# The first 18 key slots of a Perceiver cross attention: keys projected in quarters, queries in small pieces

## The chip, the cores and the metric

The kernel runs on one core of a Trainium2 chip. The metric is the device time of one execution in microseconds (us), the median of several runs. A core has five engines that matter here: TensorE (PE in the profile, with PEld for its weight loads), VectorE (DVE), ScalarE (ACT), GpSimd (POOL), and SyncE (SP), whose queue issues most of the transfers.

## What is computed

The program is one block of a Perceiver: cross attention from 512 tokens to a context of 8192, then a windowed self attention, then a mixture of experts. Only the first part is touched. Cut to that:

```python
x: (2, 512, 512)   ctx: (2, 8192, 512)   mask: (2, 1, 1, 8192)   # float32; 16 heads of 32
def xattn(query, key, value, mask, Wq, bq, Wk, bk, Wv, bv, Wo, bo):
    q, k, v = query @ Wq.T + bq, key @ Wk.T + bk, value @ Wv.T + bv
    q, k, v = split_heads(q), split_heads(k), split_heads(v)
    att = einsum('bhqd,bhkd->bhqk', q, k) / sqrt(32)
    att = where(mask == 0, -inf, att)
    out = einsum('bhqk,bhkd->bhqd', softmax(att, axis=-1), v)
    return merge_heads(out) @ Wo.T + bo
x = x + xattn(layernorm(x), ctx, ctx, mask, ...)
x = x + window_attention(layernorm(x), ...)
x = x + experts(layernorm(x), ...)
```

## The kernel before

**Units, slots and rounds.** The cross attention is cut into 8 units: 2 batches by 4 groups of 4 heads (4 x 32 = 128 rows of the array). A unit goes through the 8192 context tokens in 16 chunks (NKC) of 512 tokens (KC). Unit by unit, chunk by chunk, this gives 128 slots (NS). The main loop (L399) runs over slots, and each slot has four rounds `i`, one for each 128 queries of the batch.

A softmax needs the maximum of a row of scores before its exponentials. The kernel makes it in a pass of its own, ahead: `max_part(s, c)` (L265) computes the scores of 128 queries by 512 keys for four heads and reduces them to one maximum per query and head. The second pass, `scores` and `values` (L323, L348), begins LAG = 18 slots later. So slots 0 to 17 hold the first pass only: key projections, scores with their maxima, and the query projections that later units need. That stretch is what the change is about.

**max_part in the early slots** (L271 to L290). A score tile `sx` is two PSUM banks (2 x 512 float32), and a round uses two of them, from a pool `pairs` of three. Four float32 matmuls (L276) multiply the four heads in four strips of 32 rows of the array; four small bfloat16 matmuls (L282) subtract the mask's row, in the same tiles. Two VectorE reductions (L287), one a tile, then take the maxima. Only after that is a tile free for the next scores.

**project_k(slot, half)** (L230) projects half a chunk of keys: 16 matmuls with 32 columns of weights each, so that the four heads of the group lie in four 32-partition strips of one PSUM tile `pk`, and one ScalarE instruction (L243) adds the bias and writes `kt`. Rounds 0 and 1 of a slot do one half each (L421), after the round's `max_part`. The keys of a slot are scored in the slot after it.

**query(b, g)** (L170) projects the 512 queries of one batch for one group: four matmuls with 128x128 weights and 512 tokens (L173), and one ScalarE instruction (L177). `query_norm(b)` takes the layer norm's statistics on VectorE, and `query_in(b, c)` normalizes 128 tokens (L90), transposes them on TensorE (L98) and copies them out of PSUM on ScalarE (L99). For batch 0 the inputs and the first group come ahead of the loop (L387 to L390). All the rest is a list `later` of 12 calls, of which round 3 of slots 1 to 12 takes one each (L423).

**mask_rows** (L183) turns the mask into a bias and into rows: one VectorE instruction, two TensorE transposes, small ScalarE copies, and three small transfers to memory that ScalarE issues. SP then loads such a row, spread over 128 partitions, for each slot (L221). The first of these loads waits until the row has been written.

**PSUM.** It has eight banks. In the early slots the pool `ps` has two of them, for all of keys, queries, transposes and the maximum's column, and `pairs` has six. From slot 18 on, one pool of eight takes their place (L402).

**Order.** Each engine works through its own instructions in one order, and a framework adds the waits. That order is nearly the code's. The framework also gives out buffers, and it may put an instruction ahead of earlier ones on its engine where it reckons that those can't start yet: the statistics of batch 1, which the list asks for in slot 4, start at 18.77 us in the trace. Loads of the context (`load`, L204) are asked for one slot ahead and run up to three ahead, since four buffers take them; SP waits for a buffer at its head and holds what is behind it.

The pieces that set the order around the change:

```python
load(0); load_x(1); wv_sb = load_w(wv, cp, "wv_sb")
query_norm(0); [query_in(0, c) for c in range(4)]; query(0, 0)
mask_rows(); load_mask(0)
for slot ...:                       # L399
    for i in range(4):
        max_part(slot - 1, i)       # then scores, values from slot 18 on
        if i < 2: project_k(slot, i)
        if i == 3 and slot > 0 and later: later.pop(0)()
        if i >= 2 and slot >= NKC: project_v(slot, i - 2)
    # at a unit's last chunk: max_finish
```

Of the kernel before, what the change touches and what calls it, by code (L numbers as in the profile page):

```python
# [10 lines left out]
F32 = mybir.dt.float32  # L11
# [3 lines left out]
AF = mybir.ActivationFunctionType  # L15
ALU = mybir.AluOpType
AX = mybir.AxisListType
PSUM = bass.MemoryType.PSUM

P = 128  # L20
B, S, D = 2, 512, 512
T = B * S
S2 = 8192
H, DK = 16, 32
G = 4
DC = D // P
# [8 lines left out]
KC = 512  # L35
NKC = S2 // KC
# [7 lines left out]
def perceiver_kernel(  # L44
# [8 lines left out]
    nc = tc.nc  # L53
# [8 lines left out]
    def load_x(b):  # L62
        nc.sync.dma_start(
            out=x_sb[:, ts(b, NT // B), :],
            in_=x[ts(b, S), :].rearrange("(n p) d -> p n d", p=P),
        )
# [27 lines left out]
    def transposed(dst, src, ps):  # L94

        tp = ps.tile([P, 4, P], F32, tag="ps", name="tp")
        for c in range(4):
            nc.tensor.transpose(tp[:, c, :], src[:, ts(c, P)], ident)  # L98
        nc.scalar.copy(dst, tp)  # L99
# [17 lines left out]
    with ExitStack() as es:  # L117
        cp = es.enter_context(tc.tile_pool(name="a_const", bufs=1))
        tmp = es.enter_context(tc.tile_pool(name="a_tmp", bufs=2))
# [3 lines left out]
        pp = es.enter_context(tc.tile_pool(name="a_p", bufs=4))  # L123
        dram = es.enter_context(tc.tile_pool(name="a_dram", bufs=1, space=bass.MemoryType.DRAM))

        first_ps = ExitStack()
        ps = first_ps.enter_context(tc.tile_pool(name="a_ps1", bufs=2, space=PSUM))
        pairs = first_ps.enter_context(tc.tile_pool(name="a_pairs", bufs=3, space=PSUM))

        def load_w(src, pool, tag):  # L130
            t = pool.tile([P, DC, D], F32, tag=tag, name=tag)
            nc.sync.dma_start(out=t, in_=src.rearrange("(c p) f -> p c f", p=P))
            return t

        bq_c = cp.tile([P, G], F32, name="bq_c")
# [15 lines left out]
        nc.vector.memset(mrep, 0.0)  # L151
        junk = cp.tile([P, KC], BF16, name="junk")

        wq_sb = load_w(wq, pp, "p")
        wk_sb = load_w(wk, cp, "wk_sb")


        qT = cp.tile([P, G, T], F32, name="qT")
        xnT, ln = {}, {}

        def query_norm(b):
            ln[b] = layernorm_stats(tmp, range(b * (NT // B), (b + 1) * (NT // B)))
            xnT[b] = pp.tile([P, DC, S], F32, tag="p", name="xnT")

        def query_in(b, c):
            xn = tmp.tile([P, D], F32, tag="row", name="xn")
            normalized(xn, b * (NT // B) + c, *ln[b])
            transposed(xnT[b][:, :, ts(c, P)], xn, ps)

        def query(b, g):  # L170
            pq = ps.tile([P, S], F32, tag="ps", name="pq")
            for c in range(DC):
                nc.tensor.matmul(  # L173
                    pq, lhsT=wq_sb[:, c, ts(g, P)], rhs=xnT[b][:, c, :],
                    start=(c == 0), stop=(c == DC - 1),
                )
            nc.scalar.activation(qT[:, g, ts(b, S)], pq, AF.Identity, bias=bq_c[:, g : g + 1])  # L177

        mbias = cp.tile([P, B, S2 // P], F32, name="mbias")
        mrow = dram.tile([B, S2 // P, P], F32, name="mrow")  # L180
# [2 lines left out]
        def mask_rows():  # L183


            nc.vector.tensor_scalar(mbias, mask_i, 0.0, -BIG, ALU.is_equal, ALU.mult)
            for b in range(B):
                tp = ps.tile([P, P], F32, tag="ps", name="tpk")
                nc.tensor.transpose(tp[0 : S2 // P, :], mbias[:, b, :], ident)
                mt = tmp.tile([S2 // P, P], F32, name="mt")  # L190
                nc.scalar.copy(mt, tp[0 : S2 // P, :])
                nc.scalar.dma_start(out=mrow[b], in_=mt)
                if b == 0:
                    mh = tmp.tile([S2 // P, P], BF16, name="mh")
                    nc.scalar.mul(mh, tp[0 : S2 // P, :], -1.0)
                    nc.scalar.dma_start(out=mrow_h, in_=mh)
# [3 lines left out]
        NS = len(chunks)  # L200
# [3 lines left out]
        def load(slot):  # L204

            for b, j in {(units[u][0], j) for u, j in wanted(slot)}:
                t = ctxp.tile([P, DC, KC], F32, tag="ctx", name="ctx_t")
                nc.sync.dma_start(
                    out=t, in_=ctxT[b, :, ts(j, KC)].rearrange("(c p) s -> p c s", p=P)
                )  # L210
                ctx_t[slot, b] = t

        def load_mask(slot):

            u, j = chunks[slot]
            early = slot + 1 < LAG
            t = mp.tile(
                [P, KC], BF16 if early else F32, tag="mkh" if early else "mk", name="mk", bufs=3
            )
            rows = mrow_h if early else mrow[units[u][0]]  # L220
            nc.sync.dma_start(  # L221
                out=t,
                in_=rows[ts(j, KC // P), :].rearrange("c p -> (c p)").partition_broadcast(P),
            )
            mk_t[slot] = t
# [1 line left out]
        def wanted(slot):  # L227
            return [chunks[s] for s in (slot, slot - NKC) if 0 <= s < NS]

        def project_k(slot, half):  # L230
            u, j = chunks[slot]
            b, g = units[u]
            if half == 0:
                k_t[slot] = kp.tile([P, KC], F32, tag="k", name="kt")
            hs = ts(half, KC // 2)
            pk = ps.tile([P, KC // 2], F32, tag="ps", name="pk")
            for c in range(DC):
                for h in range(4):
                    nc.tensor.matmul(  # L239
                        pk[ts(h, DK), :], lhsT=wk_sb[:, c, ds(g * P + h * DK, DK)],  # L240
                        rhs=ctx_t[slot, b][:, c, hs], start=(c == 0), stop=(c == DC - 1),
                    )
            nc.scalar.activation(k_t[slot][:, hs], pk, AF.Identity, bias=bk_c[:, g : g + 1])  # L243
# [61 lines left out]
        def max_finish(u):  # L305


            rest = ps.tile([P, 4, 4], F32, tag="ps", name="mcol")
            nc.vector.tensor_reduce(rest, mst[u], AX.X, ALU.max)
            for i in range(3):  # L310
                nc.vector.tensor_copy(mrep[:, :, :, i], rest)
                if i < 2:
                    nc.vector.tensor_tensor(rest, rest, mrep[:, :, :, i], ALU.subtract)
            pm = ps.tile([P, S], F32, tag="ps", name="pm")
            for c in range(4):
                nc.tensor.matmul(
                    pm[:, ts(c, P)], lhsT=mrep[:, c, :, :].rearrange("p h r -> p (h r)"),
                    rhs=ident_h, start=True, stop=True,
                )
            m_t[u] = mp.tile([P, S], BF16, tag="mT", name="mT")  # L320
            nc.scalar.copy(m_t[u], pm)
# [60 lines left out]


        load(0)
        load_x(1)
        wv_sb = load_w(wv, cp, "wv_sb")
        query_norm(0)  # L387
        for c in range(NT // B):
            query_in(0, c)
        query(0, 0)  # L390
        mask_rows()
        load_mask(0)
        later = [lambda g=g: query(0, g) for g in range(1, G)]
        later += [lambda: query_norm(1)]
        later += [lambda c=c: query_in(1, c) for c in range(NT // B)]
        later += [lambda g=g: query(1, g) for g in range(G)]

        waiting = None
        for slot in range(NS + LAG):  # L399
            if slot == LAG:  # L400
                first_ps.close()
                ps = es.enter_context(tc.tile_pool(name="a_ps", bufs=8, space=PSUM))  # L402
            if slot + 1 < NS + NKC:
                load(slot + 1)
            elif slot + 1 == NS + NKC:
                wo_sb = load_w(wo, ctxp, "ctx")
                wqkv_t = [load_w(wqkv[:, ts(i, D)], ctxp, "ctx") for i in range(3)]
            if slot + 1 < NS:
                load_mask(slot + 1)
            s = slot - LAG  # L410
            for i in range(4):
                if 1 <= slot <= NS:
                    max_part(slot - 1, i)
                if s >= 0:
                    scores(s, i)
                if waiting is not None:
                    values(*waiting)
                waiting = (s, i) if s >= 0 else None
                if s >= NKC and chunks[s][1] == 1:
                    finish(chunks[s][0] - 1, i)  # L420
                if i < 2 and slot < NS:  # L421
                    project_k(slot, i)
                if i == 3 and slot > 0 and later:  # L423
                    later.pop(0)()
                if i >= 2 and NKC <= slot < NS + NKC:
                    project_v(slot, i - 2)
            if 1 <= slot <= NS and chunks[slot - 1][1] == NKC - 1:
                max_finish(chunks[slot - 1][0])
# [23 lines left out]
    ps = ctx.enter_context(tc.tile_pool(name="c_ps", bufs=8, space=PSUM))  # L452
# [21 lines left out]
    xnT, aT, hT = {}, {}, {}  # L474
# [468 lines left out]
```

## Time and profile before

| | before |
|---|---|
| median of 3 runs | 3846.05 us |
| lowest and highest | 3838.11 and 3847.68 us |
| profiled execution, its own time | 3841.49 us |
| its span in the profile | 3839.5 us |
| its mean granted TensorE clock | 0.993 |
| VectorE, ScalarE, GpSimd busy | 60%, 41%, 54% of the span |
| first scores of slot 1 (start) | 25.63 us |
| first scores of slot 16 | 224.66 us |
| first scores of slot 18 | 259.93 us |

A page of the profile shows one execution: busy time by engine, the span in 40 slices, the chain that ended last, and groups of instructions by line. The trace behind it can be asked for the instructions in order of time, for who waited for whom, and for busy time and granted clock in any stretch. A group's line gives engine, operation, output and input tiles, count, busy us and mean ns, then the idle time of the engine just before these instructions and what ended it. A float32 matmul or weight load is recorded as two instructions, so that "x32" in a row about `pk` is 16 matmuls.

The early slots are about 7% of the span (slot 18 starts at 259.93 of 3839.5 us).

### The profile page before, as it was taken

The numbers are of one execution on the slowest core, as the hardware profiler recorded it, in microseconds if no ns is written. First come the engines' busy times: TensorE is split into PE (matmuls) and PEld (weight loads), VectorE is DVE, ScalarE is ACT, GpSimd is POOL, SyncE is SP. The second block draws the span as 40 slices with busy tenths as digits, with TensorE's granted clock in tenths as the row PEclk, the third lists the DMA queues.
The fourth block names the chain that finished last, engine by engine and source line by source line (L and its number), as shares of the span: only waits on it lengthen the run. The fifth ranks groups of instructions, "written<-read, shape, count | busy, mean of one in ns | idle before, by whom it ended". The sixth has DMA issues, their size and how long they took to land.

```text
span 3839.5 us, 99475 instructions
## 1 busy us (share of the span) xinstructions
PE 3773.4 (98%) x43100; PEld 1867.9 (49%) x43100; DVE 2284.6 (60%) x5444; ACT 1588.4 (41%) x2805; POOL 2069.1 (54%) x531
## 2 busy tenths in 40 slices
PE   8999999999999999999999999999999999999998
PEld 3345554554554554555555455444555444444444
DVE  6677777777777777777777777899743500000000
ACT  1125555555555555555555555676442001111110
POOL 0019998998998998999899899500100000000000
PEclk9999999999999999999999999999999999999999
DMA  5222212222223332222122222122201168888885
GB/s 188 87 73 71 69 60 70 71 71 71 71 68 103 125 125 92 70 71 71 57 71 71 71 71 70 60 86 63 75 31 36 58 229 286 285 287 287 288 285 172
DMA packets 143735, 438.07 MB, mean 114 GB/s; under 512 B 9408, under 2 KB 11728, under 8 KB 117856
## 3 DMA queue, kind: packets, MB, share of 16 engines
q1 hardware_dynamic: 137856, 419.33, 32.7%
q0 software_dynamic: 5200, 12.30, 1.3%
q8 instruction: 337, 5.52, 0.6%
q14 instruction: 102, 0.84, 0.1%
q10 hardware_dynamic: 240, 0.08, 0.0%
HBM read 423.21 MB, written 8.47 MB: 112 GB/s over the span
## 4 chain that ended last, share of the span: by engine, by line
PE 88%; DVE 2%; issue 1%; ACT 1%; DMA 0%; POOLq 0%; DVEq 0%; SPq 0%; ACTq 0%
PE av L353 13%; PE sx L295 12%; PE sc L331 12%; PE pv L255 11%; PE pf L839 11%; PE pk L239 10%; PE py L857 5%; PE pf L780 3%; PE sc L337 3%; PE pqkv L535 2%; PE po L106 1%; PE pso L798 1%; PE tp L98 1%; PE pow L630 1%; DVE junk L300 1%
## 5 line engine op out<-in xcount | busy, mean ns | idle before, releaser
L365 POOL TENSOR_TENSOR acc<-acc,pt 128x2048 f32<-128x2048 f32 x437 | 1991.2, 4557 | 452.0 <-ACT pt L344 451.2
L344 ACT ACTIVATE pt<-sc,mbias 128x512 f32<-128x512 f32 x2016 | 1218.3, 689 | 952.3 <-PE sc L337 950.9
L300 DVE CUSTOM_DVE_ANT_0 junk<-sx,mk 128x512 bf16<-128x512 f32 x1776 | 1228.1, 691 | 550.0 <-PE sx L295 352.7
L331 PE MATMUL sc<-qT,kt 32*128 32x512 f32 x4096 | 546.5, 594 | 0.0
L353 PE MATMUL av<-pt,vt 128*32 128x512 f32 x4032 | 540.6, 605 | 2.8 <-DVE mst L300 2.8
L255 PEld LDWEIGHTS pv<-wv_sb,ctx_t 128*32 128x32 f32 x16384 | 457.6, 110 | 155.0 <-DVE mst L300 101.4
L295 PE MATMUL sx<-kt,qT 32*128 32x512 f32 x3552 | 509.3, 640 | 0.9 <-DVE vt L260 0.9
L239 PE MATMUL pk<-ctx_t,wk_sb 128*32 128x256 f32 x8192 | 499.4, 385 | 2.1 <-DVE mst L300 2.1
L255 PE MATMUL pv<-wv_sb,ctx_t 128*32 128x128 f32 x16384 | 495.0, 273 | 1.3 <-DVE avs L361 1.3
L839 PE MATMUL pf<-wt,xinT 128*128 128x512 f32 x1024 | 460.9, 595 | 1.1
L239 PEld LDWEIGHTS pk<-ctx_t,wk_sb 128*32 128x32 f32 x8192 | 264.3, 111 | 298.1 <-DVE mst L300 104.7
L361 DVE TENSOR_TENSOR avs<-av,avs 128x512 f32<-128x512 f32 x504 | 345.6, 686 | 2.8 <-PE av L353 2.5
L331 PEld LDWEIGHTS sc<-qT,kt 32*128 32x128 f32 x4096 | 245.8, 185 | 200.8 <-issue 160.1
L846 DVE TENSOR_TENSOR eo<-pf,sg 128x512 f32<-128x512 f32 x64 | 44.3, 692 | 468.7 <-PE pf L839 468.7
L839 PEld LDWEIGHTS pf<-wt,xinT 128*128 128x128 f32 x1024 | 193.9, 191 | 222.0 <-issue 213.6
L822 POOL DMA_INDIRECT xin<-h_dram,idx x16 | 15.9, 992 | 444.2 <-PE tp L98 291.6
L863 POOL DMA_INDIRECT out_x<-y,idx x16 | 25.3, 1579 | 408.8 <-DVE y L862 408.8
L353 PEld LDWEIGHTS av<-pt,vt 128*32 128x32 f32 x4032 | 81.8, 108 | 325.8 <-DVE mst L300 281.0
L857 PE MATMUL py<-wt,eoT 128*128 128x512 f32 x512 | 222.3, 592 | 0.0
L844 ACT ACTIVATE sg<-pf 128x512 f32<-128x512 f32 x64 | 38.2, 597 | 422.1 <-PE pf L839 422.1
L337 PE MATMUL sc<-mT,neg 32*128 32x512 bf16 x2048 | 207.9, 374 | 0.0
L295 PEld LDWEIGHTS sx<-kt,qT 32*128 32x128 f32 x3552 | 140.0, 183 | 138.1 <-DVE mst L300 92.3
(161 smaller groups left out, 2504.6 us busy)
## 6 DMA issues: line engine op xcount, KB each, us to landing
ctx_t<-in_ctxT SPq DMA_DIRECT2D x160, 1024.0 KB, 6.0
wt<-in_gw SPq DMA_DIRECT2D x64, 1024.0 KB, 4.9
wt<-in_up SPq DMA_DIRECT2D x64, 1024.0 KB, 4.9
wt<-in_down SPq DMA_DIRECT2D x64, 1024.0 KB, 6.5
mk<-mrow SPq DMA_DIRECT2D x111, 256.0 KB, 3.5
ctx<-in_wqkv SPq DMA_DIRECT2D x3, 1024.0 KB, 5.3
mk<-mrow_h SPq DMA_DIRECT2D x17, 128.0 KB, 2.8
x_sb<-in_x SPq DMA_DIRECT2D x2, 1024.0 KB, 10.4
```

Of the source, the lines that this page charges most:

```text
L239: nc.tensor.matmul(pk[ts(h, DK), :], lhsT=wk_sb[:, c, ds(g * P + h * DK, DK)], rhs=ctx_t[slot, b][:, c, hs], start=(c == 0), stop=(c == DC ...
L255: nc.tensor.matmul(pv[ts(k, DK), i, :], lhsT=ctx_t[slot, b][:, c, ds((2 * half + i) * P + k * DK, DK)], rhs=wv_sb[:, c, ts(g, P)], start=( ...
L295: nc.tensor.matmul(sm, lhsT=qT[r, g, ds(b * S + c * P, P)], rhs=k_t[s][r, :], start=True, stop=True)
L300: nc.vector.tensor_tensor_reduce(out=junk, in0=ss[h], in1=mk_t[s], scale=1.0, scalar=-3.0e38, op0=ALU.add, op1=ALU.max, accum_out=mst[u][: ...
L331: nc.tensor.matmul(sc, lhsT=k_t[s][r, ts(ch, P)], rhs=qT[r, g, ts(b, S)], start=True, stop=False)
L337: nc.tensor.matmul(ss[h], lhsT=neg[r, :], rhs=m_t[u][r, :], start=False, stop=True)
L344: nc.scalar.activation(pt[:, h, :], ss[h], AF.Exp, bias=mbias[:, b, cc : cc + 1], scale=SCALE)
L353: nc.tensor.matmul(av[ts(h, DK), :], lhsT=v_t[s][:, ch, ts(h, DK)], rhs=pt_t[s, ch][:, h, :], start=True, stop=True,)
L361: nc.vector.tensor_tensor(avs[u], av, avs[u], ALU.add)
L365: eng.tensor_tensor(acc[u], acc[u], pt_t[s, ch], ALU.add)
L839: nc.tensor.matmul(pf, lhsT=xinT[:, c, :], rhs=wt[:, c, :], start=False, stop=(c == DC - 1))
L857: nc.tensor.matmul(py, lhsT=eoT[:, fq * 4 + c, :], rhs=wt[:, c, :], start=False, stop=(fq == FQ - 1 and c == 3),)
```

## The change

It touches slots 0 to 17 and what comes ahead of them:

- **Keys in quarters.** Through slot 15, `project_k` works on 128 tokens instead of 256, one quarter a round. The last three quarters of a slot's keys are projected in rounds 0 to 2 of that slot, and the first quarter in round 3 of the slot before. Slots 16 and later keep halves in rounds 0 and 1.
- **Queries in pieces.** `query` takes one chunk of 128 input rows and 256 tokens. It uses 32-column weights in four strips, as `project_k` does, instead of 128x128 weights. Eight such pieces make a query projection, and every four of them share one accumulation in PSUM, over four rounds. The list `later` gets 61 items, and each round of each slot takes one, from slot 0 on.
- **PSUM banks.** `ps` (keys, values) has one bank instead of two, and a new pool `ps_q` has one for queries and transposes. The column of maxima in `max_finish` moves from PSUM to ordinary memory.
- **Order at the start.** The key weights and the first context chunk are loaded ahead of the query weights. The mask's rows are made ahead of the query inputs. The first slot's keys are projected ahead of the first queries.

```diff
-        ps = first_ps.enter_context(tc.tile_pool(name="a_ps1", bufs=2, space=PSUM))
+        ps = first_ps.enter_context(tc.tile_pool(name="a_ps1", bufs=1, space=PSUM))
+        ps_q = first_ps.enter_context(tc.tile_pool(name="a_psq", bufs=1, space=PSUM))
...
-        wq_sb = load_w(wq, pp, "p")
         wk_sb = load_w(wk, cp, "wk_sb")
...
-            transposed(xnT[b][:, :, ts(c, P)], xn, ps)
-
-        def query(b, g):
-            pq = ps.tile([P, S], F32, tag="ps", name="pq")
-            for c in range(DC):
-                nc.tensor.matmul(
-                    pq, lhsT=wq_sb[:, c, ts(g, P)], rhs=xnT[b][:, c, :],
-                    start=(c == 0), stop=(c == DC - 1),
-                )
-            nc.scalar.activation(qT[:, g, ts(b, S)], pq, AF.Identity, bias=bq_c[:, g : g + 1])
+            transposed(xnT[b][:, :, ts(c, P)], xn, ps_q)
+
+        pq = {}
+
+        def query(b, g, half, c):
+
+            if c == 0:
+                pq[0] = ps_q.tile([P, S // 2], F32, tag="ps", name="pq")
+            for h in range(4):
+                nc.tensor.matmul(
+                    pq[0][ts(h, DK), :], lhsT=wq_sb[:, c, ds(g * P + h * DK, DK)],
+                    rhs=xnT[b][:, c, ts(half, S // 2)], start=(c == 0), stop=(c == DC - 1),
+                )
+            if c == DC - 1:
+                nc.scalar.activation(
+                    qT[:, g, ds(b * S + half * (S // 2), S // 2)], pq[0], AF.Identity,
+                    bias=bq_c[:, g : g + 1],
+                )
...
-                tp = ps.tile([P, P], F32, tag="ps", name="tpk")
+                tp = (ps, ps_q)[b].tile([P, P], F32, tag="ps", name="tpk")
...
-        def project_k(slot, half):
+        def project_k(slot, part, parts=2):
             u, j = chunks[slot]
             b, g = units[u]
-            if half == 0:
+            if part == 0:
                 k_t[slot] = kp.tile([P, KC], F32, tag="k", name="kt")
-            hs = ts(half, KC // 2)
-            pk = ps.tile([P, KC // 2], F32, tag="ps", name="pk")
+            hs = ts(part, KC // parts)
+            pk = ps.tile([P, KC // parts], F32, tag="ps", name="pk")
...
-            rest = ps.tile([P, 4, 4], F32, tag="ps", name="mcol")
+            rest = tmp.tile([P, 4, 4], F32, name="mcol")
...
         load(0)
+        wq_sb = load_w(wq, pp, "p")
         load_x(1)
         wv_sb = load_w(wv, cp, "wv_sb")
+        mask_rows()
+        load_mask(0)
         query_norm(0)
         for c in range(NT // B):
             query_in(0, c)
-        query(0, 0)
-        mask_rows()
-        load_mask(0)
-        later = [lambda g=g: query(0, g) for g in range(1, G)]
+        for i in range(4):
+            project_k(0, i, 4)
+        halves = [(half, c) for half in range(2) for c in range(DC)]
+        for half, c in halves:
+            query(0, 0, half, c)
+        later = [lambda g=g, p=p: query(0, g, *p) for g in range(1, G) for p in halves]
         later += [lambda: query_norm(1)]
         later += [lambda c=c: query_in(1, c) for c in range(NT // B)]
-        later += [lambda g=g: query(1, g) for g in range(G)]
+        later += [lambda g=g, p=p: query(1, g, *p) for g in range(G) for p in halves]
...
-                ps = es.enter_context(tc.tile_pool(name="a_ps", bufs=8, space=PSUM))
+                ps = ps_q = es.enter_context(tc.tile_pool(name="a_ps", bufs=8, space=PSUM))
...
-                if i < 2 and slot < NS:
+                if slot < NKC:
+
+                    if i < 3 and slot > 0:
+                        project_k(slot, i + 1, 4)
+                    elif i == 3 and slot + 1 < NKC:
+                        project_k(slot + 1, 0, 4)
+                elif i < 2 and slot < NS:
                     project_k(slot, i)
-                if i == 3 and slot > 0 and later:
+                if later:
                     later.pop(0)()
```

## The prediction, made before the change was run

> **What bounds the kernel now.** I read the page first, then the groups of the first 262 us, then the timeline of one slot, then stretches of 4 us with their clock. The page alone says that TensorE (PE) is busy nearly all the time, which hides the point[...].
>
> ```profile
> PE 3773.4 (98%) x43100; PEld 1867.9 (49%) x43100; DVE 2284.6 (60%) x5444; ACT 1588.4 (41%) x2805; POOL 2069.1 (54%) x531
> ```
>
> The groups of the first 262 us (columns: count, busy us, mean ns, idle before and its releaser) show two engines that hand work to and fro:
>
> ```profile
> L287 DVE TENSOR_REDUCE mst<-sx 128x2 f32<-128x1024 f32 x136 | 160.3, 1221 | 71.0 <-PE sx L282 69.0
> L276 PE MATMUL sx<-kt,qT 32*128 32x512 f32 x544 | 105.7, 666 | 8.0 <-DVE mst L287 6.9 <-ACT kt L243 0.6
> L276 PEld LDWEIGHTS sx<-kt,qT 32*128 32x128 f32 x544 | 30.8, 192 | 55.2 <-DVE mst L287 29.2 <-issue 24.5 <-ACT kt L243 1.1
> ```
>
> VectorE (DVE) sat idle 69.0 us for scores, and the score weights waited 29.2 us for VectorE: neither sets the pace throughout. One slot on the timeline (start us, duration, engine, line) says why:
>
> ```profile
> 43.50 1.14 PE L276 MATMUL sx<-kt,qT 32*128 32x512 f32 x8
> 44.46 0.40 PE L282 MATMUL sx<-mk,neg 1*128 1x512 bf16 x4
> 44.79 1.93 PE L239 MATMUL pk<-ctx_t,wk_sb 128*32 128x256 f32 x32
> 46.65 1.14 PE L276 MATMUL sx<-kt,qT 32*128 32x512 f32 x8
> 48.03 4.83 DVE L287 TENSOR_REDUCE mst<-sx 128x2 f32<-128x1024 f32 x4 [0.80 <-PE sx L282]
> 49.31 0.19 PEld L276 LDWEIGHTS sx<-kt,qT 32*128 32x128 f32 x2 [1.29 <-DVE mst L287]
> 50.59 3.70 PE L173 MATMUL pq<-xnT,p 128*128 128x512 f32 x8
> 54.22 1.14 PE L276 MATMUL sx<-kt,qT 32*128 32x512 f32 x8
> 55.60 2.36 DVE L287 TENSOR_REDUCE mst<-sx 128x2 f32<-128x1024 f32 x2 [2.74 <-PE sx L282]
> ```
>
> Rounds 0 and 1 carry half a key projection each and last 3.15 us (43.50 to 46.65): 1.28 for scores and mask, 1.87 for keys. VectorE, with two reductions, needs 2.42 (half of 4.83) and idles. Rounds 2 and 3 carry nothing else: from 46.65 to 50.59 they take 3.94, where 2 x 1.28 = 2.56 is work; 1.38 is waiting for VectorE to free a score buffer. Then one whole query projection takes 3.63 while VectorE idles 2.74. Sum 2 x 3.15 + 3.94 + 3.63 = 13.87, and the slot did last 13.88. The stretches (busy us by engine, then the granted clock) show a second price:
>
> ```profile
> 76.00:80.00 4.00, 3.42 (x20) 1.02 (x18) 3.88 (x4) 0.00 (x0) 0.00 (x0) 0.97 0.76 255
> 80.00:84.00 4.00, 4.00 (x30) 1.25 (x30) 2.98 (x3) 0.00 (x0) 0.00 (x0) 0.50 0.08 23
> 156.00:160.00 4.00, 3.54 (x16) 1.13 (x13) 3.88 (x4) 0.00 (x0) 0.00 (x0) 1.00 0.78 260
> 244.00:248.00 4.00, 4.00 (x34) 1.39 (x32) 2.36 (x2) 0.00 (x0) 0.00 (x0) 0.50 0.21 80
> ```
>
> Where a slot without a query lets rounds 2, 3 and the next 0 follow each other, the clock falls to half for some 6 us; where a query fills the place (156 to 160 us) it stays whole.
>
> [...] key projections of 1.93 us take 3.64 at 81.77 and 133.82, after starved rounds. [...] 32 records of 128x32 weights with 256 tokens advance TensorE by 1.87 us where one alone lasts 385 ns. [...] two key halves back to back (21.38, x64) last 3.66 and one lasts 1.93, so a half is 1.73 of streaming, and the step of 1.87 holds 0.14 that each visit pays.
>
> **The change, part by part.** The 18 early slots have 72 rounds; slot 1 begins at 25.63, slot 16 at 224.66 and slot 18 at 259.93.
>
> *Keys in quarters.* A quarter has as many matmuls as a half, with 128 tokens instead of 256. Streaming is 1.73 / 2 = 0.865; that short pieces cost no more per token is shown by the value projections (64 records of 128 columns at 235.12 move TensorE on by 1.88, the same work in 1.87 above). With the 0.14 of a visit: 1.00.
>
> *Queries in pieces.* A piece is one chunk of 128 rows, four strips, 256 tokens: a quarter of a key half, 1.73 / 4 = 0.43. It comes right after the key quarter in the same tiling, so I add 0.04 rather than another 0.14; bounds 0.43 and 0.57. Eight pieces are 3.8 against 3.63 now: pure TensorE work rises slightly. ScalarE gets two evacuations a query for one, and four of keys for two; it is busy about 1.4 of 13.9 us in a slot, so that is hidden.
>
> *A round with a query piece* is 1.28 + 1.00 + 0.47 = 2.75 on TensorE (2.71 to 2.85) against 2.42 on VectorE. TensorE sets it, and the score buffer is back in time: the first reduction starts 1.38 after the scores and lasts 1.22, so its buffer is free at 2.60, before 2.75. The key bank is single now: its evacuation (0.47 for a half, less for a quarter) has until the next round's scores and mask are through, 1.28 and more. Both are covered; the first by only 0.15, and if that goes the round grows by the shortfall.
>
> *Slots 1 to 15.* The list has 24 + 1 + 4 + 32 = 61 items; slot 0 takes 4, so 57 rounds remain. 52 with a piece: 52 x 2.75 = 143.0. Four with a transposed input: 1.28 + 1.00 + 0.70 (93.04 to 93.74) = 2.98 each, 11.9. The one with statistics, already run at 18.77 us in the trace, and the three left in slot 15 fall to VectorE's pace: 4 x 2.43 (six reductions in 7.30) = 9.7. Sum 164.6 against 224.66 - 25.63 = 199.0: **34.4 less**. Cross-check: 15 stalls of 1.38 are 20.7, and the lost clock in slots 5, 6, 9 and 14 (15.45 x 0.23 + 14.18 x 0.23 + 17.30 x 0.20 + 13.10 x 0.13) is 12.2; together 32.9.
>
> *Before slot 1.* Slot 0 gains four query pieces and a key quarter: 1.9 + 1.0 = 2.9 later. The mask's transposes leave the place between query and keys (20.1 to 21.38): 1.3 earlier. Query transposes now share one bank: the second set could start only at 12.22, when the first copy is out, so 1.78 a set, 17.5 instead of 14.87 for all: 0 to 2.6, as keys may fill in; I take 1.3. Key quarters in one bank wait for ScalarE three times by up to 0.55 (0.47, what a half's evacuation takes, and the hand-over): 0 to 1.7, take 0.9. Two query halves: 0 to 0.7, take 0.3. If the mask's VectorE step is put ahead of the normalization it waits for its load (3.55 + 6.7 = 10.25 against 9.74): up to 0.5, in the upper bound alone. ScalarE gets the mask's three copies (0.24, 0.27, 0.26) and the three transfers that it issues (0.49, 0.55, 0.45), 2.26 in all, ahead of the first copy of queries; they can run from about 10.9, and that copy is wanted at 11.56: 0 to 1.6, take 0.8. SP's queue: first keys move ahead of query weights, one 1024 KB load (about 2.7 us) sooner; the mask row's store and load come ahead of transfers that are already queued, so nothing waits. Sum **+4.9** (+1.6 to +8.7).
>
> *Slots 16 and 17* keep halves. The single bank makes the second value projection wait until VectorE has taken the first: that ends 4.16 after the round's start, and TensorE wants the bank at 3.15 + 1.28 = 4.43; hidden by 0.27, else up to 1 us in four places. The half clock at the start of slot 16 (15.52 x 0.11 = 1.7) should go; that after the maximum's chain (243 to 250) stays. The maximum column in ordinary memory instead of a bank: nothing. **-1.7** (-5 to +4).
>
> *After slot 18* the code is the same, TensorE sets the pace, and transfers run three slots ahead, so the shift is passed on whole.
>
> Sum -34.4 + 4.9 - 1.7 = -31.2. Against the profiled execution's own 3841.49 (span 3839.5) that is 3810.3. The runs' median is 3846.05, 4.6 above it, so I predict **3815**.
>
> **Rivals.** *A smaller gain*: each piece pays its own 0.14, key quarters pay more than 1.00, and the start is serial. 52 x 0.2 = 10 and 3 at the start leave about 18: 3828. For it: single banks throughout; against: the back-to-back rates above. *The order is not what the code says*: the framework moved statistics from slot 4 to 18.77 us, so it can move pieces too; if they bunch up, the stalls stay and only mask and start shift: about 3844. Against it: all score, key and query matmuls of the slot above stand in code order. *Slower*: the clock. If a single bank holds TensorE up in each round, [...]whole rounds run at half clock, 2.75 more each; 12 such rounds (33 us) eat the gain, and 20 of 60 give 55 - 31 = +24: 3870. For it: starved rounds do lose the clock now. Against it: each early round gets about 2.3 us or more of work for 2.43 to 2.75.
>
> **How the numbers follow.** Forecast 0.81, smaller gain 0.10, order 0.05, slower 0.04. About 0.3% (11.5 us) is what a measurement can tell from no change. Faster is the first two, 0.91; same 0.05; slower 0.04. Range: rounds (-2 to +5), start (-3.3 to +3.8), slots 16 and 17 (-3.4 to +5.7), and some 5 of scatter among the runs, not all at once: 3800 to 3830, which takes in the smaller gain.
>
> **What would show it.** Right: steps of about 2.75 from one score group to the next in slots 1 to 15, VectorE's idle after each pair about 0.3, no wait of score weights for VectorE over 0.3, the clock at 1.00 from 40 us until slot 16 ends, slot 1's scores near 30.5, slot 18's near 229. Wrong: steps over 2.9 with key or query matmuls waiting for ScalarE, half clock inside slots 1 to 15, or a shift of slot 18 that doesn't reach the end.

## The result, and the profile after

| | before | after | forecast |
|---|---|---|---|
| median of the runs compared | 3842.62 us (9 runs) | 3853.76 us (9 runs) | 3815 |
| lowest and highest | 3834.79 and 3847.68 | 3848.49 and 3857.27 | 3800 to 3830 |
| profiled execution (span) | 3841.49 (3839.5) | 3853.76 (3851.7) | 3810.3 |
| first scores of slot 1 | 25.63 | 32.56 | near 30.5 |
| first scores of slot 16 | 224.66 | 195.14 | |
| first scores of slot 18 | 259.93 | 228.65 | near 229 |

The changed kernel is slower by 11 us: 1.0034 times the time before, with a 95% interval of 1.0024 to 1.0044. (The experiments below give their ratios in the same way, each against executions of the kernel before that were made beside it.) Yet slot 18 begins 31.3 us sooner, as forecast. So the gain was made and then given back, and more, after slot 18, where the prediction had said that nothing changes.

First the early part. The page's busy line looks like that of before, with 98% for TensorE again:

```profile
PE 3764.9 (98%) x44572; PEld 1885.2 (49%) x44572; DVE 2316.1 (60%) x5444; ACT 1601.5 (42%) x2845; POOL 2068.3 (54%) x531
```

The groups of the first 262 us of the changed kernel (columns as before):

```profile
L296 DVE TENSOR_REDUCE mst<-sx 128x2 f32<-128x1024 f32 x136 | 160.3, 1221 | 38.7 <-PE sx L291 38.2
L285 PE MATMUL sx<-kt,qT 32*128 32x512 f32 x544 | 82.0, 648 | 0.1
L285 PEld LDWEIGHTS sx<-kt,qT 32*128 32x128 f32 x544 | 22.8, 184 | 27.5 <-DVE mst L296 22.0 <-issue 5.3
```

VectorE's idle time ahead of the reductions fell from 71.0 to 38.7 us, and the score matmuls, 544 records in both kernels, are recorded as busy for 82.0 instead of 105.7 us. One round on the changed kernel's timeline (here and below, lines of a timeline that play no part are left out):

```profile
43.48 1.14 PE L285 MATMUL sx<-kt,qT 32*128 32x512 f32 x8
44.77 1.08 PE L248 MATMUL pk<-ctx_t,wk_sb 128*32 128x128 f32 x32
44.87 2.36 DVE L296 TENSOR_REDUCE mst<-sx 128x2 f32<-128x1024 f32 x2 [0.38 <-PE sx L291]
45.67 0.61 PE L178 MATMUL pq<-xnT,p 128*32 128x256 f32 x8
46.22 1.14 PE L285 MATMUL sx<-kt,qT 32*128 32x512 f32 x8
```

Scores, a key quarter, a query piece, and the next scores 2.73 us after the first (43.48 to 46.22, rounded): the forecast was 2.75. VectorE idles 0.38 a round. The windows of 4 us of the changed kernel (busy us by engine, then the granted clock, DMA share and GB/s) show where the clock is whole and where it is not:

```profile
80.00:84.00 4.00, 4.00 (x96) 2.45 (x92) 3.26 (x3) 0.37 (x1) 0.00 (x0) 1.00 0.03 6
212.00:216.00 4.00, 4.00 (x28) 1.23 (x28) 2.36 (x2) 0.48 (x1) 0.00 (x0) 0.52 0.41 159
526.00:530.00 4.00, 2.55 (x16) 1.35 (x20) 2.15 (x7) 0.59 (x1) 0.42 (x1) 0.53 0.21 81
```

At 80 us, where before had 0.50, it is 1.00. At 212 it is halved after the first unit's maximum, as it was at 244 before. But 526 us is deep in the part that the change was not to touch. That place is the end of the second unit, and the timeline of the changed kernel there is the key to the whole result:

```profile
521.49 0.42 DVE L318 TENSOR_REDUCE mcol<-mst 128x16 f32<-128x256 f32 x1
521.92 4.49 POOL L374 TENSOR_TENSOR acc<-acc,pt 128x2048 f32<-128x2048 f32 x1 [0.33 <-ACT pt L353]
521.94 4.53 DVE L320 CAST mrep<-mcol 128x16 bf16<-128x16 f32 x1
526.51 0.18 DVE L322 TENSOR_TENSOR mcol<-mcol,mrep 128x16 f32<-128x16 f32 x1
526.73 0.20 DVE L320 CAST mrep<-mcol 128x16 bf16<-128x16 f32 x1
527.45 0.61 PE L325 MATMUL pm<-ident_h,mrep 128*128 128x128 bf16 x4 [5.43 <-DVE mrep L320]
```

The first cast of 16 elements a partition lasts 4.53 us, the second 0.20. The long one began 0.02 us after an addition on GpSimd (POOL), and ended 0.06 us after that did. The same place in the kernel before:

```profile
552.94 0.43 DVE L309 TENSOR_REDUCE mcol<-mst 128x16 f32<-128x256 f32 x1
553.30 4.51 POOL L365 TENSOR_TENSOR acc<-acc,pt 128x2048 f32<-128x2048 f32 x1 [0.32 <-ACT pt L344]
553.87 0.22 DVE L311 CAST mrep<-mcol 128x16 bf16<-128x16 f32 x1
554.12 0.18 DVE L313 TENSOR_TENSOR mcol<-mcol,mrep 128x16 f32<-128x16 f32 x1
555.11 0.40 PE L316 MATMUL pm<-ident_h,mrep 128*128 128x128 bf16 x4 [1.71 <-DVE mrep L311]
```

The same GpSimd addition runs, and the cast beside it takes 0.22. The difference is where `mcol` lies: in PSUM before, in ordinary memory (SBUF) after. TensorE waits for the row `pm` 5.43 us instead of 1.71, and its clock halves for 6.8 us, from 526.2 on, while it still waits. The distances from one unit to the next (start of the copy that begins each unit's `avs`, in us, from the traces) show the cost at each unit end:

```
before   315.4  316.3  316.2  316.2  316.2  316.2  304.2
after    321.6  321.8  323.0  321.9  321.4  322.8  310.6
longer     6.2    5.5    6.8    5.7    5.2    6.6    6.4   = 42.4
```

-31.3 at slot 18, then +42.4 over seven unit ends, makes +11.1; the profiled spans differ by +12.2, and the 1.1 between the two lies behind the start of the last unit. The eighth unit end, the first in time, has no price: GpSimd's additions only start with the second pass, after slot 18.

### The profile page after: what moved, and what is told of

It reads as the page before. It is cut to its first block, busy times and chain, and to the rows that moved or that the text cites. A ratio compares the mean times of both kernels' runs of the same rounds, so it can differ in the third digit from the quotient of the medians.

```text
span 3851.7 us, 102451 instructions
## 1 busy us (share of the span) xinstructions
PE 3764.9 (98%) x44572; PEld 1885.2 (49%) x44572; DVE 2316.1 (60%) x5444; ACT 1601.5 (42%) x2845; POOL 2068.3 (54%) x531
## 4 chain that ended last, share of the span: by engine, by line
PE 88%; DVE 3%; issue 1%; ACT 1%; DMA 0%; POOLq 0%; DVEq 0%; SPq 0%; ACTq 0%
PE av L362 13%; PE sx L304 12%; PE sc L340 12%; PE pv L264 11%; PE pf L859 11%; PE pk L248 10%; PE py L877 5%; PE pf L800 3%; PE sc L346 3%; PE pqkv L555 2%; PE po L106 1%; PE pso L818 1%; DVE mrep L320 1%; PE tp L98 1%; DVE junk L309 1%
## 5 line engine op out<-in xcount | busy, mean ns | idle before, releaser
L248 PE MATMUL pk<-ctx_t,wk_sb 128*32 128x256 f32 (+1 forms) x9216 | 501.6, 358 | 5.2 <-DMA ctx_t<-in_ctxT 3.0
L248 PEld LDWEIGHTS pk<-ctx_t,wk_sb 128*32 128x32 f32 x9216 | 284.7, 110 | 301.3 <-DVE mst L309 104.6
L252 ACT ACTIVATE kt<-pk,bk_c 128x256 f32<-128x256 f32 (+1 forms) x288 | 129.8, 451 | 224.1 <-PE pk L248 224.0
```

The source lines that it names most:

```text
L248: nc.tensor.matmul(pk[ts(h, DK), :], lhsT=wk_sb[:, c, ds(g * P + h * DK, DK)], rhs=ctx_t[slot, b][:, c, hs], start=(c == 0), stop=(c == DC ...
```

## The experiments

**Theories.** *Held up* (mine): a VectorE instruction that works on ordinary memory alone is held up as long as GpSimd's addition runs (the cast of 4.53 us beside the addition of 4.49), and the move of `mcol` into memory is the whole loss. *Rivals*: the early gain itself brings the loss (units start at other times against the transfers, and something collides later); the new start order or the single banks cost it; or the wait for the row `pm` is the cost, whatever its cause.

**1. The change with the column back in PSUM.**

```diff
-            rest = tmp.tile([P, 4, 4], F32, name="mcol")
+            rest = ps_q.tile([P, 4, 4], F32, tag="ps", name="mcol")
```

> The change, but with the column of maxima back in a PSUM bank. Theory (VectorE and GpSimd block each other in ordinary memory): the 4.5 us instruction at the end of units 2 to 8 is gone, and with it the half clock behind it; the seven steps of 5.2 to 6.7 us that the trace shows (42.4 in all) vanish: about 3811, some 31 below the kernel before. Rival (the steps come from something else that the change does to the later slots, such as the order of instructions or the pools): the column makes no difference, about 3853.

Measured: 3807.81 us against 3840.96 for the kernel before, 0.9913 (0.9898 to 0.9928). Timeline of this kernel at the same unit end:

```profile
518.19 4.52 POOL L374 TENSOR_TENSOR acc<-acc,pt 128x2048 f32<-128x2048 f32 x1 [0.33 <-ACT pt L353]
518.75 0.22 DVE L320 CAST mrep<-mcol 128x16 bf16<-128x16 f32 x1
519.01 0.18 DVE L322 TENSOR_TENSOR mcol<-mcol,mrep 128x16 f32<-128x16 f32 x1
519.99 0.40 PE L325 MATMUL pm<-ident_h,mrep 128*128 128x128 bf16 x4 [1.70 <-DVE mrep L320]
```

The addition is there, the cast is short, the wait is 1.70, and no half clock follows. The units last what they lasted before (315.4, 316.3, 316.2 us and so on). One line was the loss: with it undone the change gains 33 us, where the prediction had 31 (how near that is, is in part luck; see below). The rival of a later collision falls, since the units start just as early here.

**2. The kernel before with the column in memory.** The same line alone, in the other direction.

```diff
-            rest = ps.tile([P, 4, 4], F32, tag="ps", name="mcol")
+            rest = tmp.tile([P, 4, 4], F32, name="mcol")
```

> The kernel before, with one line changed: the column of maxima in ordinary memory. Theory: +42 on the kernel before, about 3885, with one VectorE instruction of about 4.5 us at seven unit ends. Rival: no difference, about 3843.

Measured: 3881.78 against 3840.96, 1.0102 (1.0083 to 1.012): 41 us slower. The tile `mcol` in this kernel (durations in ns: least, median, largest; then who waited for it, us and times):

```profile
L311 DVE CAST mrep<-mcol x24: 194/202/4540, 248.2 to 2493.2; 128x16 bf16<-128x16 f32 x24
L313 DVE TENSOR_TENSOR mcol<-mcol,mrep x16: 183/184/4521, 248.4 to 2493.0; 128x16 f32<-128x16 f32 x16
...
  PE pm L316: 39.5, 8
```

39.5 us of waiting, the very sum of the changed kernel, without any other part of the change. The distances between its units add up to 41.2 us more than in the kernel before. So the loss needs neither the start order nor the single banks. The largest subtraction is as long as the largest cast: both kinds are held up. At six unit ends it is the first cast; at the last one it is the first subtraction.

**3. The change with the casts on ScalarE.** It was to ask whether the subtractions, which stay on VectorE, are held up when the casts are elsewhere.

```diff
-                nc.vector.tensor_copy(mrep[:, :, :, i], rest)
+                nc.scalar.copy(mrep[:, :, :, i], rest)
```

> The change with its column in ordinary memory, but the three copies of it made by ScalarE; VectorE keeps the two subtractions, whose inputs both lie in ordinary memory. If only the copies block each other with GpSimd: the long instruction is gone, and the time falls to about 3812 to 3820. If an instruction with two inputs in ordinary memory blocks as well (the trace has one such subtraction of 4.52 us at the last unit): a subtraction becomes the long one and the time stays at 3845 to 3860. Rival that the column doesn't matter: 3853.

Measured: 3825.12, 0.996 (0.9945 to 0.9975). Timeline of this kernel:

```profile
518.33 0.26 ACT L320 CAST mrep<-mcol 128x16 bf16<-128x16 f32 x1 [5.05 <-DVE mcol L318]
518.62 0.18 DVE L322 TENSOR_TENSOR mcol<-mcol,mrep 128x16 f32<-128x16 f32 x1 [0.33 <-ACT mrep L320]
519.46 2.41 ACT L353 ACTIVATE pt<-sc,mbias 128x512 f32<-128x512 f32 x4
522.02 4.53 POOL L374 TENSOR_TENSOR acc<-acc,pt 128x2048 f32<-128x2048 f32 x1 [4.05 <-ACT pt L353]
```

The chain is short, but this does not answer the question. ScalarE's first cast waits at the head of its queue (5.05 us), the exponentials stand behind it until 519.46, and so GpSimd's addition starts only at 522.02, when the chain is done. Nothing overlaps, so nothing could be held up. The run costs 17 us more than the first experiment. The wait put ahead of the exponentials is a likely cause, with two half clocks of 6.8 us behind it (at 521.8 and 842.7); that was not tried on its own.

**4. One addition moved to VectorE, behind the chain.** With nothing on GpSimd at that moment, the casts should be short with the column still in memory.

```diff
-            if not first:
+            if j == NKC - 2 and ch == 2 and s + LAG <= NS:
+                moved.append((u, s, ch))
+            elif not first:
...
+                while moved:
+                    u, s, ch = moved.pop()
+                    nc.vector.tensor_tensor(acc[u], acc[u], pt_t[s, ch], ALU.add)
```

> The change with its column in ordinary memory, but the one addition per unit that GpSimd does beside the chain of maxima is done by VectorE after that chain, so that GpSimd is free meanwhile. Theory: all VectorE instructions of the chain are short again, no half clock at the unit ends, 7 x 6 us less, 7 x (0 to 2.2) us more for the addition on VectorE: 3811 to 3828. Rival (ordinary memory itself is slow for such a column, or the order is at fault): 3853 or more.

Measured: 3864.01, 1.006 (1.0041 to 1.0078), slower than the change itself. I had picked the addition one round too early: the next one still met the chain. Timeline of this kernel:

```profile
520.17 0.20 DVE L320 CAST mrep<-mcol 128x16 bf16<-128x16 f32 x1
520.33 4.50 POOL L376 TENSOR_TENSOR acc<-acc,pt 128x2048 f32<-128x2048 f32 x1 [6.75 <-ACT pt L353]
520.41 4.45 DVE L322 TENSOR_TENSOR mcol<-mcol,mrep 128x16 f32<-128x16 f32 x1
```

My expectation failed, but the miss answers what the third run left open. The cast, begun before the addition, is short; the subtraction, begun 0.08 us after it, lasts 4.45. So it is not the cast as such: whichever cast or subtraction of the chain comes after the start of the addition is held until its end.

**5. The right addition moved.**

```diff
-                eng = nc.gpsimd if s + LAG <= NS else nc.vector
+                eng = nc.gpsimd if s + LAG <= NS and (j, ch) != (NKC - 2, 3) else nc.vector
```

> The change with its column in ordinary memory, but the addition that the trace shows beside the chain (the fourth round's, which the run before this one missed by one round) is done by VectorE, right behind the chain. Theory: the whole chain is short, in copies and subtractions, with the column still in ordinary memory; 7 x 6 us less and 7 x (0 to 2.3) more for VectorE's extra work: 3808 to 3826. Rival (the column in ordinary memory costs by itself): 3845 or more.

Measured: 3816.25 against 3840.99, 0.9937 (0.9922 to 0.9952). Timeline of this kernel:

```profile
517.78 0.20 DVE L320 CAST mrep<-mcol 128x16 bf16<-128x16 f32 x1
518.02 0.18 DVE L322 TENSOR_TENSOR mcol<-mcol,mrep 128x16 f32<-128x16 f32 x1
519.38 2.28 DVE L374 TENSOR_TENSOR acc<-acc,pt 128x2048 f32<-128x2048 f32 x1
```

The column is still in memory, only GpSimd's addition is gone, and the chain is as short as with PSUM. This is the other half of the proof: memory alone costs nothing, memory beside GpSimd does. (At the last unit end another addition of GpSimd's is still running when the first cast begins, and that cast lasts 0.82 us, to the addition's end.) The 8 us that this run lacks to the first experiment fit the addition on VectorE, 2.28 us a unit: six of the seven units grow by 1.2 to 1.3.

**6. The first experiment with the start order of before** (query inputs and first queries ahead of the mask's rows and the first keys; query weights loaded first).

```diff
+        wq_sb = load_w(wq, pp, "p")
         wk_sb = load_w(wk, cp, "wk_sb")
...
         load(0)
-        wq_sb = load_w(wq, pp, "p")
...
-        mask_rows()
-        load_mask(0)
         query_norm(0)
         for c in range(NT // B):
             query_in(0, c)
-        for i in range(4):
-            project_k(0, i, 4)
         halves = [(half, c) for half in range(2) for c in range(DC)]
         for half, c in halves:
             query(0, 0, half, c)
+        mask_rows()
+        load_mask(0)
+        for i in range(4):
+            project_k(0, i, 4)
```

> The version with the column in PSUM, and the order of the start as in the kernel before (query weights first, queries before keys, mask rows between). The forecast priced the new start at +4.9 with the 2.9 of added work in it; the trace of the change shows TensorE waiting 3.0 us for the first context chunk while the query inputs were ready. If the new order costs that wait: slot 1 starts at about 29 instead of 31.9 and the time is some 3 us less than with the new order, about 3805. If the new order helps by getting the mask off the path: slot 1 starts at 33 or later and the time is 1 to 3 us more.

Measured: 3807.99, 0.9919 (0.9905 to 0.9932), the same as the first experiment. Slot 1 starts 1.5 us sooner (30.36 against 31.87) and so does slot 16 (192.94 against 194.44), but the first copy into `avs` comes at 233.74 against 233.62: a half clock of 3.4 us at 211.2 takes it back. The start order is worth nothing that these runs show.

**7. The first experiment with whole queries**: all eight pieces in round 3 of slots 1 to 12, keys in quarters.

```diff
+        whole = lambda b, g: [query(b, g, *p) for p in halves]
-        later = [lambda g=g, p=p: query(0, g, *p) for g in range(1, G) for p in halves]
+        later = [lambda g=g: whole(0, g) for g in range(1, G)]
...
-        later += [lambda g=g, p=p: query(1, g, *p) for g in range(G) for p in halves]
+        later += [lambda g=g: whole(1, g) for g in range(G)]
...
-                if later:
+                if i == 3 and slot > 0 and later:
```

> The version with the column in PSUM, keys in quarters in every round, but a whole query projection (its eight pieces) at once in round 3 of slots 1 to 12, where the kernel before had it. If the spread of the keys gives most of the gain: three rounds at VectorE's pace of 2.43 and one of 2.3 + 3.8 or so, 13 a slot with a query and 9.8 without, about 4 to 8 us slower than the version with pieces: 3812 to 3816. If the pieces give most of it: stalls stay and it is near 3835.

Measured: 3825.94, 0.9964 (0.9951 to 0.9977), 10 to 14 us more than I expected where the quarters give most of the gain. Timeline of this kernel:

```profile
40.32 1.91 PE L178 MATMUL pq<-xnT,p 128*32 128x256 f32 x32
43.21 1.93 PE L178 MATMUL pq<-xnT,p 128*32 128x256 f32 x32
46.45 9.78 DVE L296 TENSOR_REDUCE mst<-sx 128x2 f32<-128x1024 f32 x8 [4.75 <-PE sx L291]
```

I had left out the single query bank: the second half waits until ScalarE has emptied it, the next scores go partly in between, and VectorE then idles 4.75 us (2.74 in the kernel before). A slot with a query lasts 14.5 us, the others around 10.5. With these banks, the pieces are worth 18 us beside the quarters.

**8. The first experiment with keys in halves**, in rounds 0 and 1, queries in pieces.

```diff
-                if slot < NKC:
-
-                    if i < 3 and slot > 0:
-                        project_k(slot, i + 1, 4)
-                    elif i == 3 and slot + 1 < NKC:
-                        project_k(slot + 1, 0, 4)
-                elif i < 2 and slot < NS:
+                if i < 2 and 0 < slot < NS:
                     project_k(slot, i)
```

> The version with the column in PSUM, queries in pieces, one a round, but keys in halves in rounds 0 and 1 of their slot as in the kernel before. Rounds 0 and 1 take about 3.6 on TensorE, rounds 2 and 3 fall to VectorE's 2.43: 12.0 a slot against 10.9, so 10 to 16 us slower than the version with quarters: 3818 to 3824. If the quarters don't matter once the pieces are spread: 3808 to 3811.

Measured: 3830.14, 0.9977 (0.9967 to 0.9986), again above what I expected. Timeline of this kernel, a round with a key half and the two after it:

```profile
48.77 1.93 PE L248 MATMUL pk<-ctx_t,wk_sb 128*32 128x256 f32 x32
48.87 2.36 DVE L296 TENSOR_REDUCE mst<-sx 128x2 f32<-128x1024 f32 x2 [1.41 <-PE sx L291]
52.45 7.30 DVE L296 TENSOR_REDUCE mst<-sx 128x2 f32<-128x1024 f32 x6 [1.23 <-PE sx L291]
```

Rounds with a half take about 3.6 us and leave VectorE idle for 1.2 to 1.4; the rounds without are set by VectorE. A slot lasts 12.3 us, against 10.9 with quarters. Quarters without pieces (run 7, with its waits for the single query bank) gain 15 us on the kernel before, pieces without quarters (run 8) 11, both together 33. That fits the view that the two need each other, since a round is even only when both its loads are; whole queries with two banks were not tried.

**9 and 10. The row built a round later**, to test whether the wait for `pm` is the cost. `max_finish` is cut after the casts; the rest, `max_row` (the `pm` matmuls and their copy), is called in round 1 of the next slot. Run 9 has the column in PSUM, run 10 in memory.

```diff
+        def max_row(u):
             pm = ps.tile([P, S], F32, tag="ps", name="pm")
...
+                if i == 1 and 2 <= slot <= NS + 1 and chunks[slot - 2][1] == NKC - 1:
+                    max_row(chunks[slot - 2][0])
```

> The version with the column in PSUM, and the two-step end of a unit taken apart: VectorE's chain stays at the end of the slot, but TensorE's matmuls that turn the column into a row come two rounds later (nothing needs the row before the next slot but one). In the version with the column in PSUM TensorE still waits 13.3 us in 8 unit ends for VectorE's chain. If that wait is what the chain costs: 8 to 13 us less, about 3795 to 3800. If VectorE's 1.9 us of chain cost the time wherever the row is made (it holds up the reductions behind it): no change, 3806 to 3809.

> The change, column in ordinary memory, with the same two rounds of delay for TensorE's matmuls. VectorE still stands still for 4.5 us at seven unit ends beside GpSimd's addition. If the loss goes through TensorE's wait for the row and the clock that halves in it: most of the 42 us goes, 3800 to 3818. If VectorE's standstill itself holds TensorE up, since the scores' banks don't come free: TensorE waits elsewhere, and the time stays at 3835 to 3853.

Measured: run 9 3804.18, 0.9902 (0.9885 to 0.9919), the fastest of all, 3.6 us below the first experiment, where I had expected 8 to 13 or nothing. TensorE's 13.3 us of waits for the row in the first experiment were thus worth a few us at most. The intervals of the two ratios overlap; the single times (3803.91 to 3804.94, and 3807.12 to 3809.26) do not, but they come from two chips, so even the 3.6 is not sure. Run 10: 3851.82, 1.0028 (1.0018 to 1.0038), no better than the change. Timeline of run 10:

```profile
516.91 4.50 POOL L376 TENSOR_TENSOR acc<-acc,pt 128x2048 f32<-128x2048 f32 x1 [0.33 <-ACT pt L355]
516.93 4.54 DVE L320 CAST mrep<-mcol 128x16 bf16<-128x16 f32 x1
523.00 1.55 PE L342 MATMUL sc<-qT,kt 32*128 32x512 f32 x3 [4.08 <-DVE avs L372]
```

TensorE no longer waits for the row, but 4.08 us for a bank that VectorE empties late. So the rival about the row falls: the cost is VectorE's standstill of 4.5 us, and TensorE runs out of banks soon after, whatever it was to do next.

## Why the prediction was wrong

**The step that failed** is this one: "The maximum column in ordinary memory instead of a bank: nothing." With it fell the sentence after it, that past slot 18 "the code is the same": `max_finish` runs at each of the eight unit ends, seven of them beside GpSimd's additions. Measured, the nothing was +42.4 us over seven unit ends, +41 in the kernel before (run 2).

**Mechanism, shown.** A cast or subtraction of the chain that begins while GpSimd's addition runs lasts until that ends (4.53, 4.54 us in place of 0.20, and 4.45 to 4.54 in place of 0.18), if all that it reads lies in SBUF (the change, runs 2, 4, 10); it is short if `mcol` lies in PSUM (run 1) or if the addition is gone (run 5). The kind of instruction counts too, so the theory as I put it was too wide. The last unit end of the changed kernel shows it, beside two additions in a row (the first ends at 2454.68, the second starts at 2454.76):

```profile
2450.11 9.13 POOL L374 TENSOR_TENSOR acc<-acc,pt 128x2048 f32<-128x2048 f32 x2
2453.84 0.42 DVE L318 TENSOR_REDUCE mcol<-mst 128x16 f32<-128x256 f32 x1
2454.29 0.44 DVE L320 CAST mrep<-mcol 128x16 bf16<-128x16 f32 x1
2454.77 4.52 DVE L322 TENSOR_TENSOR mcol<-mcol,mrep 128x16 f32<-128x16 f32 x1
```

The reduction reads and writes SBUF wholly inside the first addition, and takes its usual 0.42. The cast waits for the rest of that addition, the subtraction for the whole of the next one.

Of the order the runs show one side, that what began after GpSimd's addition was held: the cast that began 0.02 us after it in the change lasted 4.53 us, the subtraction that began 0.08 us after it in run 4 lasted 4.45. That a VectorE instruction which is first holds GpSimd off, no run here shows. Nor do they show why an operand in PSUM frees the cast: measured is a cast from PSUM of 0.22 us beside the addition of 4.52 in run 1. I had not asked who runs beside the chain, because I read the edit as one about banks.

**What could have been seen.** The kernel before shows the chain's casts from 553.87 on inside GpSimd's addition from 553.30 to 557.81. It even holds one meeting with GpSimd that took time: VectorE's own addition of two SBUF tiles into `acc`, never over 2.29 us elsewhere, lasts 3.13 at 2487.29, begun 0.32 us into a GpSimd multiplication of 1.29 us. That is 0.84 us too long, with 0.97 of the multiplication left to run. A question about the one line that moves, "what does this instruction read after the edit, and who else runs then?", gives, if the cast is held in the same way, an estimate from these traces: at most the addition's 4.51 us less the cast's 0.22, so 4.3 us of standstill at seven places, 30 us, and the clock on top. That takes the gain of 31 away.

**The size.** TensorE's waits for the row grew from 13.4 to 39.5 us, +26.1. The half clocks at the seven unit ends (six of 6.8 us, one of 3.4; 44.4 in all) begin while TensorE still stands idle, for 10.4 of these 44.4 us in the trace. The other 34.0 at half speed lose 17.0 us by my estimate. Together that is 43, against 42.4 measured, so these two terms account for the loss, though no run changed the clock alone. What makes the clock fall was not shown beyond this: with waits of 5.42 to 5.67 us the halving came at each of the seven places, with 1.7 us at none of them in the kernel before. (The half clock at 212 us, at the first unit's end, came with a wait of only 1.31, so the length of the wait alone does not settle it; in runs 1, 3, 5, 9 and 10 it did not come there.)

**Step by step.**
- *Key quarters, query pieces and the round of 2.75*: right, 2.73.
- *Slots 1 to 15, 164.6*: right, and 2.0 too long: 162.6 (32.56 to 195.14), from the rounds of 2.73 and from slot 15, which took 9.1 where the sum has 10.0. No half clock in them. (In the cross-check the lost clock adds up to 12.0, not 12.2; nothing rests on it.)
- *Before slot 1, +4.9*: 2.0 too low, +6.9, inside its range. One term, that in SP's queue "nothing waits", left out a wait for the first context chunk, which the changed kernel's timeline shows:

```profile
14.83 1.46 PE L248 MATMUL pk<-ctx_t,wk_sb 128*32 128x128 f32 x18 [2.99 <-DMA ctx_t<-in_ctxT]
```

  With the keys first, TensorE stands 2.99 us for data that used to come while it worked on queries. In run 6, with the old order, slot 1 begins 1.5 us sooner than in run 1, and that is worth nothing in the end. The rest of the miss is within the scatter: in the profiled executions that share the change's start (the change, runs 1, 3, 4, 5, 9, 10), slot 1 begins between 31.06 and 32.56.
- *Slots 16 and 17, -1.7*: right, -1.8 (33.5 for 35.3). The half clock at the first unit's end stayed, as the forecast said, but in run 1, where it did not come, these slots take 30.4.
- *Sum at slot 18, -31.2*: right, -31.3, and closer than its terms, which is luck: the 2.0 too much in slots 1 to 15 and the 2.0 too little before them cancel. In run 1 slot 18 begins at 224.82, 35.1 sooner than in the kernel before, and the whole time is 33 shorter.
- *The shift is passed on whole*: right in run 1, wrong in the change, for the reason above.
- *Rivals*: none of them was it. The one on the slower side had a fallen clock, but in the early rounds, from single banks; it came at the unit ends, from a column of 16 numbers. "A shift of slot 18 that doesn't reach the end" was on the list of what would show the forecast wrong, and that is how it showed.

## What to carry to other kernels

When an edit moves a small tile from PSUM to SBUF to free a bank, list every VectorE instruction that reads it, and see what GpSimd runs at that moment: a 0.2 us cast or subtraction took the length of GpSimd's whole instruction here (4.45 to 4.54 us). In the profile this does not show as a wait, it shows as a busy VectorE, so look for the largest duration of a tile's instructions beside the median (202 and 4540 ns in run 2). The chain that ended last shows it too: in the changed kernel five of these casts, 4.54 us each, are among its longest pieces. And where a change has several parts, run the one that "costs nothing" alone first: here one line decided the sign of the whole.

## What the runs showed of the hardware

- A VectorE cast or two-input instruction on SBUF alone, held by a GpSimd addition, is recorded as running the whole time: 4.53 us for 128x16 elements, ending within 0.06 us of the addition's end.
- Not all VectorE work on SBUF is held. A reduction of 128x256 to 128x16 elements took 0.42 us inside an addition as outside, and 24 reciprocals of 128x128 in place (`rl`, in the changed kernel), inside additions, took 0.89 to 0.95, as the eight others did.
- It depends on order. In run 4 a cast that began 0.16 us ahead of the addition kept its 0.20 us, and the subtraction 0.08 us after the addition's start took 4.45.
- The same addition of 128x2048 numbers lasts 2.28 us on VectorE (run 5) and some 4.5 on GpSimd.
- 32-column pieces in four strips cost what was derived from longer ones: a key quarter and a query piece beside 1.28 us of scores and mask gave a round of 2.73 us, where the sum had 2.75.
